# Two DMA streams moved from SyncE's queue to ScalarE's, and a planner that knows two TensorE clocks

## The chip, the cores and the metric

The kernel runs on one core of a Trainium2 chip. The metric is the device time of one execution in microseconds (us), as a median of several runs. A core has five engines that run side by side, each working through its own instructions in order: TensorE (PE, matrix products, with its weight loads shown as PEld), VectorE (DVE), ScalarE (ACT), GpSimd (POOL) and SyncE (SP, used here only to issue DMA transfers). They wait for each other by semaphores.

## The reference

The input x has shape 4 x 384 x 32 x 32 (batch, channels, height, width). Everything is float32. Layer 0 is a group norm followed by a selective scan in four directions; layer 1 is windowed attention and a mixture of four experts, of which each token uses two.

```
x = x + conv(group_norm(x))
    # conv: for each of 4 directions k and each of 384 channels d, with 16 states n:
    #   dt = softplus(dt_proj(x_proj(x)) + bias)
    #   h[n] = h[n] * exp(dt * A[n]) + dt * u * B[n]      (a scan over 1024 positions)
    #   y    = sum over n of h[n] * C[n]  + D * u
    # the four directions are added, then a layer norm and a gelu
t = tokens(x)                                   # 4 x 1024 tokens of 384
t = t + attention(layer_norm(t))                # 6 heads of 64, causal, 64 tokens back
t = t + experts(layer_norm(t))                  # top 2 of 4, hidden size 1536, gelu
```

## The kernel before

**The scan.** The 4 batches x 4 directions are 16 turns. A turn has 3 groups of 128 channels, and each of these is cut into 4 groups of 32. That makes 192 blocks of 32 channels. On the 128 partitions stand 32 channels times 4 states, so a block takes 4 slots for its 16 states, 768 slots in all. One slot is:

- `decay` (from line 772): ScalarE computes dA = exp(dt * A), 128 x 1024, into one of two tiles in PSUM (`das_`).
- `times_b` (756): POOL computes z = (dt * u) * B.
- `scan` (798): DVE scans h = dA * h + z along the 1024 positions.
- `times_c` (785): h is multiplied by C, on POOL or on DVE, whichever the planner thinks is free first.
- `fold_y` (828): when the four slots of a block are done, PE adds the 16 states of each channel by a product with the constant `fold` (output of 32 partitions), on top of the earlier value of y, loaded from DRAM as `yp`. ScalarE copies the sum back into `yp`, and a DMA stores it to `ydr`.

dt and dt * u are computed for 128 channels at a time by `time_steps` (689) and stored to a DRAM tile `dtr`. `spread(0)` and `spread(1)` (746) load them from there for each block of 32 channels, with each channel repeated on 4 partitions: `spread(0)` brings dt (for `decay`) into a stock of two tiles, `spread(1)` brings dt * u (for `times_b`) into another two. `state_rows` (677) loads the rows of B and C.

**Layer 1.** For each batch whose scan has ended, `front` (897), `attention` (956) and `route` (1161) run one after the other. Then `experts` (1296) runs over 19 blocks of 128 rows: for each, the hidden product (`ps_hid`, then a gelu on ScalarE into `hs`) and the output product (`y_ff`), with the weights loaded from DRAM for each block in 8 tiles. `combine` (1395) gathers the rows back. The layer 1 work of one batch is to run while the scan of the next is under way. The experts of a batch and its combination come last in priority.

**The order.** No order is written out by hand. Each of these parts is a Python generator that asks for one operation at a time, and a planner (`Machine`, line 201) decides in which order the instructions are emitted. It keeps a clock for each engine, adds a cost to it for each operation (`Engine.ask`, line 147), and remembers when each tile will be written and read. For each engine it picks, among the operations that can start by then, the one with the earliest start plus a bias (`EARLY` = -6 us, `LATER` = 6 us); for ScalarE it first prefers those that need no new activation table. The costs only decide the order; on the chip every engine runs what it was given in that order and waits where its inputs aren't there. Tiles come from stocks (`Stock.take` and `give`); three PSUM banks (`banks`) are shared by nearly all products. Planned start times of operations on SP get a margin of 1 us (`MARGIN`, `QUEUES`).

In the profile, all operations that go through `Engine.run` have line 137 and those of a list of calls (`Engine.all`) line 145.

Of the kernel before, what the change touches and what calls it, by code (L numbers as in the profile page):

```python
# [17 lines left out]
P = 128  # L18
# [50 lines left out]
class Stock:  # L69


    def __init__(self, m, pool, tag, n, shape):
        self.m, self.free = m, []
        self.tags, self.queue = {}, []
        self.add(pool, tag, n, shape)
# [32 lines left out]
class Op:  # L108


    def __init__(self, eng, outs, ins, cost, table, size):
        self.eng, self.outs, self.ins, self.cost, self.table, self.size = eng, outs, ins, cost, table, size


TABLES = {AF.Exp: "exp", AF.Ln: "ln", AF.Gelu: "gelu", AF.Sqrt: "sqrt"}
# [10 lines left out]
class Engine:  # L126
# [12 lines left out]
    def all(self, calls):  # L139

        asked = [self.ask(*c) for c in calls]
        outs, ins = ([ap for o in asked for ap in getattr(o, side)] for side in ("outs", "ins"))
        yield Op(self.name, outs, ins, sum(o.cost for o in asked), None, 0)
        for op, a, k in calls:
            getattr(self.real, op)(*a, **k)  # L145

    def ask(self, op, a, k):
        aps = [v for v in list(a) + [v for n, v in k.items() if n not in ("out", "accum_out")] if hasattr(v, "tensor")]
        if "out" in k:
            outs, ins = [k["out"]], aps  # L150
        else:
            outs, ins = aps[:1], aps[1:]
        if op == "value_load":
            outs, ins = [], aps
        if op == "tensor_tensor_reduce":
            outs, ins = outs + ins[-1:], ins[:-1]
        if k.get("accum_out") is not None:
            outs = outs + [k["accum_out"]]
        for v in list(k.values()):
            if isinstance(v, bass.IndirectOffsetOnAxis):  # L160
                ins = ins + [v.ap]
        n = max(v.free_size() if callable(v.free_size) else v.free_size for v in (outs if op == "matmul" else outs + ins))
        size, table = 0, None
        if "dma" in op:
            size = max(_nbytes(v) for v in outs + ins[:1])
            if op == "indirect_dma_start":
                size = P * D * 4
            cost = dict(pool=1.0, act=0.38, sp=0.48)[self.name]
        elif self.name == "pe":
            cost = max(n, 90) * (0.00122 if op == "transpose" else 0.00214)  # L170
            if outs[0].shape[0] == 32:
                cost *= 0.42
            if ins[0].shape[0] < 32:
                cost *= 0.6
        elif self.name == "act":
            cost = 0.08 + 0.00085 * n + 0.1 * sum(hasattr(k.get(v), "tensor") for v in ("bias", "scale"))
            cost += 0.19 if "accum_out" in k else 0.0
            table = TABLES.get(a[2]) if op == "activation" else None
        elif self.name == "pool":
            cost = 0.1 + 0.0022 * n  # L180
        elif self.name == "sp":
            cost = 1.5
        else:
            cost = 0.17 + 0.00198 * n if "scan" in op else 0.14 + 0.00105 * n
            if n < 256 and not any(v.space == PSUM for v in outs + ins):
                cost += 0.5
        return Op(self.name, outs, ins, cost, table, size)


def _nbytes(ap):  # L190
    n = 4
    for s in ap.shape:
        n *= s
    return n
# [6 lines left out]
class Machine:  # L201
# [4 lines left out]
    def __init__(self, nc):  # L206
        self.clock = dict(pe=0.0, act=0.0, dve=0.0, pool=0.0, sp=0.0)
        self.busy = dict(self.clock)
        self.written, self.read = {}, {}
        self.dram = {}  # L210
        self.dma, self.table, self.t, self.reach = 0.0, None, 0.0, 0.0
        self.pending = {e: [] for e in self.clock}
        self.waiting = []
        self.pe, self.act, self.dve = Engine(self, "pe", nc.tensor), Engine(self, "act", nc.scalar), Engine(self, "dve", nc.vector)
        self.pool, self.sp = Engine(self, "pool", nc.gpsimd), Engine(self, "sp", nc.sync)
# [31 lines left out]
    def settled(self, *tiles):  # L247

        names = [ap.tensor.name for ap in tiles]
        return lambda: max(self.written.get(n, (0.0, None))[0] for n in names) <= self.t + SOON  # L250

    def account(self, op, start):
        e = op.eng
        if op.table and op.table != self.table:
            start += TABLE_LOAD
            self.table = op.table
        end = start + op.cost
        self.busy[e] += end - max(self.clock[e], start)
        self.clock[e] = end
        if op.size:  # L260
            self.dma = max(self.dma, end) + op.size / DMA_RATE
            end = max(end + DMA_TIME, self.dma + 1.0)
            e = "dma"
        for aps, log, w in ((op.ins, self.read, False), (op.outs, self.written, True)):
            for ap in aps:
                name = ap.tensor.name
                if str(ap.space) .endswith("DRAM"):
                    self.dram.setdefault(name, []).append((*self.span(ap), end, w))
                elif log.get(name, (0.0, None))[0] <= end:
                    log[name] = end, e  # L270
        self.reach = max(self.reach, end)
# [77 lines left out]

PATIENCE = 3.0  # L350
SOON = 0.5
MARGIN, QUEUES = 1.0, ("sp",)


# [2 lines left out]
def conv_attn_hybrid(  # L357
# [146 lines left out]
    ydr = [dram.tile([T, JB, P, LQ], F32, tag="ydr", name="ydr") for _ in range(B)]  # L504
# [19 lines left out]
    pe, act, dve, pool, sp = m.pe, m.act, m.dve, m.pool, m.sp  # L524
# [221 lines left out]
    def spread(c):  # L746

        for n, (i, t, j) in enumerate(blocks):
            yield lambda: (i, t) in dtrs
            dst = yield from (dtus if c else dts).take("dts")  # L750
            yield from sp.dma_start(
                dst, dtrs[i, t][c, 32 * j : 32 * j + 32, :].unsqueeze(1).to_broadcast([32, SG, L])
            )
            spreads[n, c] = dst
# [43 lines left out]
    def scan():  # L798

        for s in range(NSLOT):  # L800
            n, g = divmod(s, NG)
            i = blocks[n][0]
            yield lambda: s in zs and s in das
            z, da = zs[s], das.pop(s)
            on_pool = count_of["times"] >= min(s + AHEAD, NSLOT) and m.clock["pool"] < m.clock["dve"] + LEAD
            h = z if on_pool else da
            if turns[i][1] >= 2:
                yield from dve.tensor_tensor_scan(
                    h[:, ::-1], da[:, ::-1], z[:, ::-1], 0.0, ALU.mult, ALU.add
                )  # L810
            else:
                yield from dve.tensor_tensor_scan(h, da, z, 0.0, ALU.mult, ALU.add)
            count_of["scan"] = s + 1
            if g == 0:
                m.spawn(fold_y(n), EARLY)
            if on_pool:
                das_.give(da)
                m.spawn(times_c(s, h, True))
            else:
                yield from times_c(s, h, False)  # L820
        ended.append(True)
        yield lambda: len(das_.free) == 2
        for stock in (banks, ybank):
            stock.free.append(das_.free.pop(0))
# [3 lines left out]
    def fold_y(n):  # L828


        i, t, j = blocks[n]
        b, k = turns[i]
        prev = yield from yps.take("yp")
        yield from sp.dma_start(prev, ydr[b][t, j])
        yield lambda: all(n * NG + g in ready for g in range(NG))
        yield m.settled(prev, *(zs[n * NG + g] for g in range(NG)))
        ps = yield from banks.take("ps_y", 0)
        y = ps[:, :LQ]
        mm = Calls()
        mm.matmul(y, ident, prev, start=True, stop=False)  # L840
        for g in range(NG):
            z = zs[n * NG + g]
            for q in range(4):
                if k % 2:
                    rhs = z.rearrange("p (w h) -> p h w", h=HH)[:, ts(q, HH // 4), :]
                else:
                    rhs = z[:, ts(q, LQ)]
                mm.matmul(y[32 * q : 32 * q + 32, :], fold, rhs, start=False, stop=g == NG - 1)
        yield from pe.all(mm)
        for g in range(NG):  # L850
            zs_.give(zs.pop(n * NG + g))
        yield from act.copy(prev, y)
        banks.give(ps)
        yield from sp.dma_start(ydr[b][t, j], prev)
        yps.give(prev)
        folded[b] = folded.get(b, 0) + 1
        if folded[b] == KG * NB:
            have.add(("scan", b))
# [656 lines left out]
```

## Time and profile before

Three runs took 4282.9, 4304.15 and 4314.34 us, median 4304.15 us. The profiled execution has a span of 4286.6 us.

| engine | busy us | share of the span | instructions |
|---|---|---|---|
| PE | 3167.0 | 74% | 19588 |
| PEld | 2064.0 | 48% | 19588 |
| DVE | 2925.7 | 68% | 2975 |
| ACT | 2293.2 | 53% | 3858 |
| POOL | 2769.1 | 65% | 1284 |

Issuing a DMA isn't counted as busy. The mean clock that PE was granted is 0.814 of full speed. The DMA engines moved 960.99 MB. In the profile a group of instructions is named by output tile, arrow, input tiles; "L137" and "L145" are the planner's lines, so the tile names tell the operations apart. A wait is written as engine, tile, arrow, and what came last before it could go on.

| DMA issues on SP | count | KB each |
|---|---|---|
| weights of the experts, `w_sb` | 608 | 576 |
| spreads, `dts` (both kinds) | 384 | 512 |
| rows of B and C, `bc` | 128 | 512 |
| loads of y, `yp` | 192 | 128 |
| stores of y, `ydr` | 192 | 128 |

A float32 product shows as two records, so 36 records of `ps_hid` are 18 products.

### The profile page before, as it was taken

What the parts mean: (1) busy time and instruction counts of PE and PEld (TensorE: products, weight loads), DVE (VectorE), ACT (ScalarE), POOL (GpSimd) and SP (SyncE); (2) the same over time, 40 slices, a digit from 0 to 9 for tenths busy, and PEclk for the clock granted to TensorE, in tenths of its full rate; (3) what the DMA queues carried; (4) which work ended last, traced back from release to release, by engine and by line L of the source; (5) the groups of instructions that cost most, each with busy time, mean ns of one, the idle gap of its engine ahead of it and who ended that gap; (6) DMA issues with size and microseconds to landing.
All of it is one profiled execution on the core that took longest, in us unless ns stands there. A gap on an engine that the chain in (4) does not pass through costs nothing.

```text
span 4286.6 us, 56954 instructions
## 1 busy us (share of the span) xinstructions
PE 3167.0 (74%) x19588; PEld 2064.0 (48%) x19588; DVE 2925.7 (68%) x2975; ACT 2293.2 (53%) x3858; POOL 2769.1 (65%) x1284
## 2 busy tenths in 40 slices
PE   2434344569955776687778856878999899998997
PEld 1111111235633443354455524545777677776785
DVE  2999999989898889998988999899621112211001
ACT  3555555676564777775667665886433234331221
POOL 1999999998888898998788988999500100002001
PEclk7566565578867898897778868889899899998997
DMA  5667563653457796765657777876349784397995
GB/s 191 208 238 237 185 231 130 195 196 122 141 193 290 259 320 216 248 237 168 214 173 272 247 242 245 310 264 213 120 127 334 266 298 126 119 335 261 309 320 168
DMA packets 450137, 960.99 MB, mean 224 GB/s; under 512 B 52980, under 2 KB 269304, under 8 KB 449848
## 3 DMA queue, kind: packets, MB, share of 16 engines
q1 hardware_dynamic: 441656, 932.17, 63.5%
q0 software_dynamic: 8192, 25.17, 1.7%
q8 instruction: 156, 2.56, 0.2%
q14 instruction: 133, 1.09, 0.1%
HBM read 805.46 MB, written 170.59 MB: 228 GB/s over the span
## 4 chain that ended last, share of the span: by engine, by line
PE 32%; DVE 10%; issue 5%; POOL 5%; ACT 5%; DMA 3%; SPq 0%; DVEq 0%; POOLq 0%; ACTq 0%
PE y_ff L145 9%; PE ps_hid L145 9%; POOL z L137 4%; DVE dA L137 4%; DVE z L137 3%; PE ps_y L145 2%; PE ps_o L145 2%; PE ps_c L145 2%; PE ps_qk L145 2%; ACT L137 1%; ACT dA L137 1%; PE ps_pr L145 1%; PE ps_p L145 1%; PE ps_v L145 1%; PE ps_s L145 1%
## 5 line engine op out<-in xcount | busy, mean ns | idle before, releaser
L137 POOL TENSOR_TENSOR z<-dts,bc 128x1024 f32<-128x1024 f32 x768 | 1797.6, 2370 | 158.6 <-ACT ps_sp L137 89.4
L137 ACT ACTIVATE dA<-dts,a 128x1024 f32<-128x1024 f32 x768 | 853.4, 1117 | 725.9 <-DVE z L137 697.3
L137 POOL TENSOR_TENSOR z<-z,bc 128x1024 f32<-128x1024 f32 x366 | 861.9, 2364 | 182.0 <-DVE z L137 161.8
L137 DVE TENSOR_TENSOR_SCAN dA<-dA,z 128x1024 f32<-128x1024 f32 x402 | 919.1, 2286 | 63.7 <-ACT dA L137 44.7
L145 PE MATMUL ps_y<-z,fold 128*32 128x256 f32 x6144 | 633.5, 556 | 303.2 <-POOL z L137 220.6
L137 DVE TENSOR_TENSOR_SCAN z<-dA,z 128x1024 f32<-128x1024 f32 x366 | 822.9, 2274 | 21.8 <-ACT dA L137 21.3
L145 PEld LDWEIGHTS ps_hid<-xbt,w_sb 128*128 128x128 f32 x5472 | 658.2, 199 | 50.2 <-issue 12.2
L145 PE MATMUL y_ff<-w_sb,hs 128*128 128x384 f32 x1824 | 662.6, 506 | 22.6 <-ACT hs L137 19.8
L145 PE MATMUL ps_hid<-xbt,w_sb 128*128 128x128 f32 x5472 | 668.7, 283 | 13.8 <-ACT dt L137 6.1
L145 PEld LDWEIGHTS ps_y<-z,fold 128*32 128x32 f32 x6144 | 203.9, 134 | 678.7 <-POOL z L137 296.6
L137 POOL DMA_INDIRECT xsdr<-tks,idx x64 | 63.3, 988 | 710.6 <-DMA tks<-tkdr 575.6
L137 DVE TENSOR_TENSOR z<-dA,bc 128x1024 f32<-128x1024 f32 x402 | 490.8, 1221 | 44.2 <-DMA bc<-xdr 22.9
L137 ACT ACTIVATE hs<-ps_hid,bb 128x128 f32<-128x128 f32 x912 | 265.7, 370 | 453.3 <-PE ps_hid L145 344.3
L145 PEld LDWEIGHTS y_ff<-w_sb,hs 128*128 128x128 f32 x1824 | 339.2, 197 | 238.7 <-issue 34.5
L145 PE MATMUL ps_y<-yp,ident 128*128 128x256 f32 x384 | 176.2, 551 | 346.7 <-ACT dt L137 172.4
L137 ACT ACT_TABLE_LOAD x315 | 404.1, 1283 | 34.4 <-DVE gs L137 11.8
L137 POOL DMA_INDIRECT cb<-ysdr,idx x64 | 62.0, 969 | 451.7 <-DMA cb<-t2dr 277.1
L145 PEld LDWEIGHTS ps_y<-yp,ident 128*128 128x128 f32 x384 | 77.6, 246 | 440.3 <-ACT dt L137 196.3
L137 DVE COPY yb<-y_ff 128x384 f32<-128x384 f32 x40 | 22.1, 554 | 299.7 <-PE y_ff L145 268.6
L145 PE MATMUL ps_dt<-xd,dtw_sb 12*128 12x512 f32 x192 | 100.2, 851 | 63.7 <-DMA dtw_sb<-in_dtw_dram 22.1
L145 PE MATMUL ps_o<-v,pt 128*128 128x64 f32 x720 | 143.8, 319 | 3.4 <-ACT pt L137 1.7
L145 PEld LDWEIGHTS ps_o<-v,pt 128*128 128x128 f32 x720 | 118.3, 207 | 31.9 <-ACT pt L137 2.6
(181 smaller groups left out, 3312.6 us busy)
## 6 DMA issues: line engine op xcount, KB each, us to landing
w_sb<-wl SPq DMA_DIRECT2D x608, 576.0 KB
dts<-dtr SPq DMA_DIRECT2D x384, 512.0 KB
bc<-xdr SPq DMA_DIRECT2D x128, 512.0 KB
ub<-udr SPq DMA_DIRECT2D x48, 512.0 KB
dtr<-e SPq DMA_DIRECT2D x48, 512.0 KB
dtr<-dt SPq DMA_DIRECT2D x48, 512.0 KB
yp<-ydr SPq DMA_DIRECT2D x192, 128.0 KB
ydr<-yp SPq DMA_DIRECT2D x192, 128.0 KB
```

Of the source, the lines that this page charges most:

```text
L137: return getattr(self.real, op)(*a, **k)
L145: getattr(self.real, op)(*a, **k)
```

## The change

It has two parts.

First, `spread` and the store at the end of `fold_y` are issued with `act.dma_start` in place of `sp.dma_start`. Both kinds of spread come from the same line, so all 384 spreads and all 192 stores of y move. The aim is to take waiting transfers out of SP's one queue.

Second, the planner's costs for PE change. Before, a product cost a fixed time per column. Now it has a cost at full clock and takes `COLD` = 1.9 times as long in a window of `WINDOW` = 3.413 us whose predecessor held less than a third of a window of work; the work of a product is counted by the share of the array's rows that it uses, and half for products with an output of 32 partitions. The aim is a plan whose PE times are nearer to the real ones, with an order that fits them.

```diff
@@ Engine.all
-        yield Op(self.name, outs, ins, sum(o.cost for o in asked), None, 0)
+        whole = Op(self.name, outs, ins, sum(o.cost for o in asked), None, 0)
+        whole.work = sum(o.work for o in asked)
+        yield whole
@@ Engine.ask
-            cost = max(n, 90) * (0.00122 if op == "transpose" else 0.00214)
+            cost = max(n, 90) * (0.00088 if op == "transpose" else 0.00176)
             if outs[0].shape[0] == 32:
-                cost *= 0.42
+                cost *= 0.51
             if ins[0].shape[0] < 32:
                 cost *= 0.6
...
-        return Op(self.name, outs, ins, cost, table, size)
+        asked = Op(self.name, outs, ins, cost, table, size)
+        if self.name == "pe":
+            asked.work = cost * min(ins[0].shape[0], P) / P if outs[0].shape[0] > 32 else 0.5 * cost
+        return asked
@@ Machine.__init__
-        self.dram = {}
+        self.dram, self.worked = {}, {}
@@ Machine.account
         end = start + op.cost
+        if e == "pe":
+
+            left, end = op.cost, start
+            while left > 0:
+                n = int(end / WINDOW)
+                f = 1.0 if self.worked.get(n - 1, 0.0) > WINDOW / 3 else COLD
+                step = min(left * f, (n + 1) * WINDOW - end + 1e-6)
+                self.worked[n] = self.worked.get(n, 0.0) + op.work * step / f / op.cost
+                left, end = left - step / f, end + step
@@ 
+WINDOW, COLD = 3.413, 1.9
@@ spread
-            yield from sp.dma_start(
+            yield from act.dma_start(
                 dst, dtrs[i, t][c, 32 * j : 32 * j + 32, :].unsqueeze(1).to_broadcast([32, SG, L])
             )
@@ fold_y
         yield from act.copy(prev, y)
         banks.give(ps)
-        yield from sp.dma_start(ydr[b][t, j], prev)
+        yield from act.dma_start(ydr[b][t, j], prev)
```

## The prediction

> **What bounds the kernel now.** I read the slices first, then the same engines by stage, then the waits of the DMA queue and the groups. The slices:
>
> ```profile
> PE   2434344569955776687778856878999899998997
> DVE  2999999989898889998988999899621112211001
> ACT  3555555676564777775667665886433234331221
> POOL 1999999998888898998788988999500100002001
> PEclk7566565578867898897778868889899899998997
> ```
>
> There are two regimes. Up to about 3070 us DVE and POOL run near full: the selective scan, 768 slots in four batches. After it PE runs near full, finishing what of attention and experts was not fitted in earlier. The stage view (stretch, then busy time of PE, weight loads, DVE, ACT, POOL, then clock) shows the size of the slack:
>
> ```profile
> 96.00:830.00 734.00, 306.68 (x1874) 95.62 (x1874) 709.16 (x483) 402.39 (x475) 702.29 (x305) 0.59 0.61 205
> 830.00:1600.00 770.00, 566.65 (x3578) 345.58 (x3577) 672.18 (x672) 508.87 (x788) 686.52 (x305) 0.81 0.62 215
> 1600.00:2340.00 740.00, 559.76 (x3565) 351.63 (x3566) 672.58 (x616) 505.08 (x794) 641.18 (x277) 0.82 0.63 214
> 2340.00:3070.00 730.00, 558.52 (x3675) 355.05 (x3674) 661.86 (x560) 495.15 (x754) 656.21 (x300) 0.84 0.71 246
> 3790.00:4230.00 440.00, 415.02 (x2454) 327.74 (x2452) 35.72 (x106) 100.22 (x320) 30.59 (x32) 0.96 0.85 292
> ```
>
> The first stage is full (DVE 709 of 734 us) and can't shrink. The next three leave DVE idle 98, 67 and 68 us: about 230 us is the most that better order could take out of the scan. PE is busy 75% there at a clock of 0.81 to 0.84, so it has room for expert work. How much it gets is seen in the windows of the output matmul alone (time, PE busy and count first):
>
> ```profile
> 830.00:1600.00 770.00, 60.07 (x168) 30.36 (x168) 1.61 (x3) 1.93 (x4) 0.81 0.62 215
> 1600.00:2340.00 740.00, 74.80 (x202) 36.94 (x203) 1.65 (x3) 2.38 (x5) 0.82 0.63 214
> 2340.00:3070.00 730.00, 121.39 (x315) 60.27 (x313) 2.73 (x5) 3.83 (x8) 0.84 0.71 246
> 3790.00:4230.00 440.00, 198.57 (x570) 106.01 (x570) 10.59 (x19) 2.39 (x5) 0.96 0.85 292
> ```
>
> A block of 128 rows takes 24 records of this matmul (1824 over 76 blocks). So 685/24 = 28.5 blocks, 38%, are done before the scan ends, and 47.5 after. In the last stage 570/24 = 23.75 blocks take 440 us: **18.5 us a block** is the price of each block left for the tail.
>
> The queue of SyncE, where all direct loads and stores now stand in one order, waits like this in the scan (total, times, longest):
>
> ```profile
> SPq L137 <- ACT yp L137: 506.4, 154, 19.0
> SPq L137 <- POOL z L137: 461.1, 176, 10.1
> SPq L137 <- ACT dA L137: 287.0, 112, 13.7
> ```
>
> The first is a store of y that waits for its copy. The second is a spread of dt * u that waits for POOL's products to free one of two buffers, the third a spread of dt that waits for the exponentials to free one. Every load behind them waits too. The engines that bound the scan see little of it: of their waits in that stretch, DVE puts 22.9 us to a load of the B and C rows, POOL 11.5 us to the same and 7.7 us to a spread.
>
> **What the Trainium skill says.** "DMA: Bandwidth & Descriptors", section "Issuing engines are not separate DMA queues": moving an issue to another engine saves only the issuing sequencer's time, since the same 16 DMA engines carry it. So I count nothing for bandwidth. The trace shows one queue row for all direct transfers, at 63.5% of the engines; a second row is not shown here. The same page, "Anatomy of one DMA": any wait happens on the issuing sequencer before dispatch. That agrees with the three rows above, and means the moved waits will now stand in ScalarE's stream. "TensorE: Matmul & The Clock Gate", Part 1: the array runs at half rate until it has been busy for a window of about 3.4 us. The trace agrees in direction: mean clock 0.59 in the first stage with little PE work, 0.96 in the last. The window itself isn't shown by the trace.
>
> **The change part by part.**
>
> *Moved issues.* Both kinds of spread come from one line, so 384 spreads and 192 stores of y leave SP for ScalarE. On SP one such issue has a median of 524 ns (spreads) and 337 ns (stores). SP loses 384 x 0.524 + 192 x 0.337 = 266 us of issuing and most of the 506 + 461 + 287 = 1254 us of waits. What was queued behind them, loads of tokens, weights, B and C rows, can go earlier. What it is worth: DVE's and POOL's waits on loads are 42 us by the rows above, and POOL waits 49.7 us for PE's folds to free z, some of which start late for a load of y (PE puts 21.0 us to that). I take half of the two, 45 us.
>
> *Cost on ScalarE.* No issue from ScalarE is in this trace. Lower end 0 (an issue hidden while an earlier activation runs). Upper end: SP's 266 us plus, for each store, a wait for the copy just before it, at most its 0.37 us (the copy group's mean) x 192 = 71 us, so 337 us. I take 266 us, 66 a stage: ScalarE goes from 68% (505 of 740) to about 77% in the full stages. Behind a stalled issue stands the next exponential, and behind that DVE's scan. A spread of dt costs no extra wait, since the exponential that frees its buffer runs on ScalarE itself. A spread of dt * u does: it waits for POOL, so ScalarE now hangs on POOL's pace wherever the real POOL runs behind the plan. But the exponentials have spare time: they sit 697 us waiting for DVE to free one of two dA buffers, and DVE waits just 44.7 + 21.3 = 66 us for them. I expose about a tenth, 30 us; at the upper end a third of 337, 112 us.
>
> *PE costs in the planner.* Old: 0.00214 us a column always. New: 0.00176 at full clock, 1.9 times that (0.00334) when the previous 3.413 us window held under a third of work. A block has 36 hidden products of 128 columns and 12 output products of 384, 9216 columns: planned 19.7 us before, 16.2 us after when warm. Measured in the trace: 36 records of the hidden product run in 4.02 us and 6 of the output in about 1.94 us, so 2 x 4.02 + 4 x 1.94 = 15.8 us warm. The old plan was 25% too slow for warm PE, and so left it idle in the real run between two folds; the new one is within 3%. A fold (32 columns out) is planned at 0.230 us in both when warm; cold it goes to 0.437 us, where 8 records (4 folds) take 1.08 us, 0.27 each. So cold folds become too dear in the plan, and this will push against experts in thin stretches. If all of the 18% that the plan thinks shorter went to experts, 28.5 blocks would become about 33.5, 5 more; I take half, 2.5 blocks x 18.5 = 46 us off the tail.
>
> *Tail order.* In 3070 to 4230 us PE is idle 260-270, 434-450, 415-440: 51 us. Loads planned with a PE that is 25% too slow come late; the pauses I saw were loads of weights around 3311, 3762 and 3770 us, 4.5 to 8 us each. I take 20 us.
>
> *The extra field and bookkeeping* run when the kernel is traced, before the chip: nothing.
>
> Sum: 4304 - 45 + 30 - 46 - 20 = 4223, say **4225 us**.
>
> **The rivals.**
>
> *Nothing gained (4295).* The scan is held by DVE and POOL work alone (709 and 702 of 734 us in the first stage), and what PE gets is set by the three PSUM banks and the order of attention, which the change leaves. For it: attention of the third batch ends only after the scan whatever the SP queue does. Against: 230 us of idle DVE isn't work. Time: 4304 - 10.
>
> *Slower (4400).* ScalarE becomes the stall: 112 us at the upper end, and little of the gains is left. For it: only two dA buffers stand between the exponentials and DVE; SP's 176 waits for POOL, 461 us, move into ScalarE's stream, where a plan that misjudges POOL turns each into a late exponential. Against: 697 us of slack. 4304 + 112 - 16 = 4400.
>
> *Much better (4110).* All 5 blocks fit in (93 us), DVE's idle time in the last three scan stages falls by a third (75 us), tail pauses go (26 us): 4304 - 194.
>
> **How the numbers follow.** Forecast 0.46, nothing gained 0.18, slower 0.21, much better 0.15. The order of some thousand instructions a stage is redone by the planner, so each case is spread by some 40 us; the three runs of before alone span 31 us. The range 4095 to 4365 takes the forecast, the middle case and most of the best, and leaves out most of the slower case and the far end of the best. Faster by over 1% (under 4261): all of the best and most of the forecast, 0.59. Within 1%: the middle case and some of the forecast, 0.21. Slower: 0.20.
>
> **What would show each step.** SP's waits on ACT yp, ACT dA and POOL z vanish and its issues fall by 576; ScalarE shows 576 issues of 0.3 to 0.55 us; DVE's waits on ACT dA stay under 100 us. More than 31 blocks of output matmuls stand before the scan's end, the scan ends by about 3050 us, and the tail falls from 1217 us to under 1170. I am wrong if DVE waits on ScalarE by 150 us or more, if the scan ends after 3100 us, or if fewer blocks than 28 fit in it.

## The result, and the profile after

The changed kernel takes 4473.39 us (median of four runs, 4465.72 to 4482.11), the kernel before 4296.47 us (4282.9 to 4314.34). The ratio is **1.041**, interval 1.0363 to 1.0457: slower by 4.1%, where 4225 us and a gain were forecast. The time lies above the range of 4095 to 4365 us.

The slices of the changed kernel:

```profile
PE   2434343568874775777777765578999999996997
DVE  3999999988889899999898979996220112221001
PEclk7556555678866886887788877788999999996997
```

The two regimes are the same, but PE's digits in the scan are lower (7s where there were 8s and 9s), and the PE-bound stretch behind it is longer. The views by stage, cut at the end of the scan (3056 us before, 3091 us after; that is where DVE starts its last instruction on `dA`), put sizes to it. What lies behind the scan is called the tail. First the kernel before, then the changed one; columns as in the prediction:

```profile
96.00:3056.00 2960.00, 1977.61 (x12555) 1137.55 (x12555) 2710.99 (x2314) 1906.91 (x2797) 2680.75 (x1182) 0.76 0.64 220
3056.00:4286.00 1230.00, 1159.58 (x6969) 913.97 (x6967) 194.36 (x615) 359.33 (x1028) 82.36 (x83) 0.93 0.69 237
```

```profile
96.00:3091.00 2995.00, 1904.89 (x11826) 1076.90 (x11827) 2717.25 (x2311) 1840.63 (x2670) 2625.83 (x1154) 0.74 0.60 206
3091.00:4473.00 1382.00, 1298.71 (x7698) 1024.70 (x7696) 213.31 (x654) 389.11 (x1119) 92.89 (x94) 0.92 0.70 237
```

The scan took 35 us longer and **the tail 152 us longer**. PE did 729 records less inside the scan, and they came back in the tail. Most of them belong to the experts, as the windows of the output matmul alone show, before and then after:

```profile
96.00:3056.00 2960.00, 256.26 (x684) 127.56 (x684) 5.98 (x11) 8.14 (x17) 0.76 0.64 220
3056.00:4286.00 1230.00, 406.33 (x1140) 211.66 (x1140) 16.17 (x29) 9.06 (x19) 0.93 0.69 237
```

```profile
96.00:3091.00 2995.00, 212.01 (x528) 104.04 (x528) 3.17 (x6) 7.67 (x16) 0.74 0.60 206
3091.00:4473.00 1382.00, 450.36 (x1296) 235.19 (x1296) 14.50 (x26) 13.38 (x28) 0.92 0.70 237
```

At 24 records a block that is 684/24 = 28.5 blocks of expert work inside the scan before and 528/24 = 22.0 after. Each engine runs in the order it was given, so this is no accident of the run: the same two numbers stand in the order that the planner wrote, in PE's stream ahead of the last fold. A block has 72 records of the hidden matmul and 24 of the output, so 6.5 blocks are 624 of the 729 records.

The moved issues did what was expected of them on their own queue. The DMA view of the changed kernel shows a second row, and the groups show 384 spreads at a median of 521 ns and 192 stores at 326 ns from ScalarE:

```profile
q1 hardware_dynamic: 358712, 705.64, 46.3%
q10 hardware_dynamic: 82944, 226.53, 14.8%
```

SP's waits (scan stretch of the changed kernel; total, times, longest) are new ones:

```profile
SPq L138 <- DVE e L138: 504.8, 46, 35.9
SPq L138 <- PE y_ff L148: 247.7, 51, 14.0
SPq L138 <- DMA ydr<-yp: 242.4, 39, 17.6
SPq L138 <- POOL z L138: 211.6, 66, 20.9
```

The two rows together hold the packets and bytes of the one row before (441656 and 932.17 MB), and they kept the 16 DMA engines busy for as long: 61.1% of 4473 us is 2733 us, and 63.5% of 4287 us was 2722 us. So the second row brought no bandwidth, as the Trainium skill has it in "DMA: Bandwidth & Descriptors", section "Issuing engines are not separate DMA queues": the transfers run on the same 16 engines, whichever engine issues them. SP's waits for the copies and the exponentials are gone. In their place SP now arrives early at stores that wait for dt * u, and at loads of y that wait for ScalarE's store of the same tile. Whether that hurts is told below by the last experiment.

### The profile page after: what moved, and what is told of

Same layout as the page of the kernel before. It is cut to its first block, busy times and chain, and to the rows that moved or that the text cites. A ratio compares the mean times of both kernels' runs of the same rounds, so it can differ in the third digit from the quotient of the medians.

```text
span 4473.3 us, 56930 instructions
## 1 busy us (share of the span) xinstructions
PE 3233.2 (72%) x19588; PEld 2114.1 (47%) x19588; DVE 2950.9 (66%) x3011; ACT 2256.0 (50%) x3820; POOL 2725.1 (61%) x1266
## 5 line engine op out<-in xcount | busy, mean ns | idle before, releaser
L138 DVE TENSOR_TENSOR_SCAN dA<-dA,z 128x1024 f32<-128x1024 f32 x420 | 960.6, 2287 | 84.4 <-ACT dA L138 69.5
L138 POOL TENSOR_TENSOR z<-z,bc 128x1024 f32<-128x1024 f32 x348 | 818.0, 2362 | 266.3 <-DVE z L138 241.0
L138 DVE TENSOR_TENSOR_SCAN z<-dA,z 128x1024 f32<-128x1024 f32 x348 | 781.8, 2274 | 22.2 <-ACT dA L138 21.5
L138 DVE TENSOR_TENSOR z<-dA,bc 128x1024 f32<-128x1024 f32 x420 | 512.6, 1221 | 35.4 <-DMA bc<-xdr 12.6
L138 ACT ACT_TABLE_LOAD x281 | 360.5, 1283 | 49.4 <-DVE gs L138 11.7
L138 DVE COPY xbt<-ps_xb 128x384 f32<-128x384 f32 x52 | 28.7, 553 | 433.8 <-PE ps_xb L148 433.8
```

Of the source, the lines that this page charges most:

```text
L138: return getattr(self.real, op)(*a, **k)
```

## The experiments

The theories, by the letters that the expectations use. **S**: ScalarE stalls on the moved issues. **C**: the cold clock in the plan does it all. **P**: what counts is how many expert blocks the order puts ahead of the scan's end, at 18.5 us each. **O**: the order costs, not the issuing engine. **F**: the overpriced cold fold makes the plan believe PE full. **K**: two clocks in a plan are bad in themselves. **R**: the order of before was tuned, and any reshuffle costs. **A**: the price of the moved issues in the plan. **N**: their lost margin. **M**: the old price of PE was a useful margin.

All ratios are to the kernel before, run on the same chip. "Blocks" are those ahead of the last fold in the order written, "scan ends" and "tail" are from each run's profile (a single execution).

| run | us | ratio (95%) | blocks | scan ends | tail |
|---|---|---|---|---|---|
| before | 4296 | 1 | 28.5 | 3057 | 1230 |
| changed | 4473 | 1.041 (1.036-1.046) | 22.0 | 3092 | 1382 |
| e1 moves alone | 4367 | 1.019 (1.015-1.024) | 23.75 | 3043 | 1312 |
| e2 PE model alone | 4412 | 1.029 (1.025-1.032) | 23.0 | 3028 | 1382 |
| e3 changed, one clock | 4380 | 1.022 (1.018-1.026) | 28.0 | 3107 | 1264 |
| e4 model, one clock | 4334 | 1.010 (1.006-1.014) | 28.5 | 3130 | 1209 |
| e5 order of before, on ScalarE | 4315 | 1.006 (1.003-1.009) | 28.5 | 3091 | 1236 |
| e6 order of changed, on SyncE | 4460 | 1.042 (1.040-1.045) | 22.0 | 3063 | 1384 |
| e7 model, fold price 0.32 | 4335 | 1.012 (1.009-1.014) | 29.75 | 3183 | 1152 |
| e8 changed, fold price 0.32 | 4451 | 1.039 (1.036-1.042) | 28.0 | 3200 | 1248 |
| e9 nudge of LEAD | 4286 | 0.999 (0.998-1.001) | 27.0 | 3024 | 1264 |
| e10 nudge of transposes | 4276 | 0.997 (0.996-0.998) | 27.5 | 3027 | 1247 |
| e11 moves free in the plan | 4364 | 1.017 (1.014-1.021) | 26.5 | 3077 | 1283 |
| e12 two clocks, dear PE | 4269 | 0.995 (0.993-0.997) | 27.25 | 3058 | 1202 |
| e13 moves with margin | 4376 | 1.020 (1.015-1.025) | 25.25 | 3090 | 1288 |
| e14 changed, dear PE | 4364 | 1.017 (1.013-1.022) | 26.5 | 3122 | 1248 |
| e15 stores alone | 4375 | 1.022 (1.017-1.026) | 25.5 | 3082 | 1281 |
| e16 spreads alone | 4382 | 1.024 (1.019-1.030) | 24.25 | 3080 | 1289 |
| e17 order of e1, on SyncE | 4352 | 1.014 (1.010-1.018) | 23.75 | 3031 | 1315 |
| e18 order of e12, on ScalarE | 4275 | 0.996 (0.995-0.998) | 27.25 | 3065 | 1213 |

### The two halves, and the clock (e1 to e4)

e1 makes only the two replacements of `sp.dma_start` by `act.dma_start` in the kernel before. e2 is the changed kernel with them undone. e3 and e4 are the changed kernel and e2 with

```diff
-WINDOW, COLD = 3.413, 1.9
+WINDOW, COLD = 3.413, 1.0
```

> Only the spreads and the stores of y are issued from ScalarE; the planner's PE costs are the old ones. In PE's emitted order 23.75 expert blocks stand ahead of the last fold (28.5 in the kernel before, 22.0 in the changed one). Theory P (placement: each expert block left behind the scan costs 18.5 us of tail): 4.75 blocks x 18.5 = 88 us over before, about 4385 us. Theory S (ScalarE stalls on the moved issues, the placement is a side effect): nearly the whole loss, about 4470 us, and the scan's end at 3095 us or later. Theory C (the cold clock in the planner does it all): about 4300 us.

> Only the new PE costs with the two clocks; all transfers stay on SyncE. 23.0 expert blocks stand ahead of the last fold. Theory P: 5.5 x 18.5 = 102 us over before, about 4400 us. Theory S: no loss, about 4300 us. Theory C: nearly the whole loss, about 4470 us.

> The changed kernel with COLD = 1.0: the new costs at full clock only, with the moved issues kept. 28.0 expert blocks stand ahead of the last fold. Theory P: 0.5 x 18.5 = 9 us over before, about 4305 us. Theory S: the loss stays, about 4450 us. Theory C: the loss goes, about 4300 us, so it is told from P by the two runs of one part alone.

> The new PE costs with COLD = 1.0, all transfers on SyncE. 28.5 expert blocks stand ahead of the last fold, 18.5 ahead of the third batch's last (14.75 before). Theory P: as before, about 4295 us, or some less since the batches before are further on. Theories S and C: about 4295 us.

Each half loses by itself, 1.9% and 2.9%, and together they lose 4.1%, about their sum (the intervals don't tell 4.1 from 4.8). C falls with e1, and S fails to explain e2, where ScalarE issues nothing. P got e1 (4367 for 4385) and e2 (4412 for 4400) nearly right, but not e3 (4380 for 4305) and e4 (4334 for 4295): there the blocks are back in the scan and the tail is short again (1264 and 1209 us), but **the scan has grown** to 3107 and 3130 us. So P tells half of it: a block put into the scan isn't free there.

### The same order, the other engine (e5, e6)

These plan a transfer for one engine and issue it from the other, so that no other instruction moves:

```diff
+        self.moved = Engine(self, "sp", nc.scalar)
...
-        yield from sp.dma_start(ydr[b][t, j], prev)
+        yield from m.moved.dma_start(ydr[b][t, j], prev)
```

and likewise for the spreads. e6 does the reverse to the changed kernel (`Engine(self, "act", nc.sync)`).

> The plan of the kernel before, with the same order on every engine, but the 384 spreads and 192 stores of y are issued from ScalarE at the places in time where the plan had them for SyncE. 28.5 blocks stand ahead of the last fold. Theory S (ScalarE stalls on the moved issues): a loss of 70 us or more, about 4370 us, with the scan's end later by as much. Theory O (the loss comes from the new order, not from the issuing engine): within 25 us of before, about 4300 us.

> The plan of the changed kernel, with the same order on every engine, but the moved transfers are issued from SyncE again. 22.0 blocks stand ahead of the last fold. Theory S: the loss from ScalarE goes, about 4400 us. Theory O: as the changed kernel or slower (SyncE has the waits back without a plan for them), 4470 to 4500 us.

S falls. 576 issues from ScalarE in an unchanged order cost 0.6%, 26 us; the order of the changed kernel costs the same 4.2% when SP issues everything. So the loss lies in the order. ScalarE's waits in e5 have two rows that the move brought (scan stretch; in the kernel before the first of these is 1.3 us and the second isn't there):

```profile
ACT dA L137 <- DMA dts<-dtr: 16.7, 5, 4.8
...
ACT dA L137 <- POOL z L137: 10.2, 3, 6.6
```

The first reads as exponentials that wait for a spread issued late, the second as exponentials behind a spread of dt * u that waits for POOL. That these two are the 26 us isn't shown: e18 (below) has 10.7 and 7.4 us in the same rows and loses nothing clear of the noise.

### What the plan believed (e7, e8)

The planner's own busy count of PE up to the last scan of the first batch (planned at 768 to 785 us), where PE does little but folds, can be set beside what PE was busy in the trace (96 to 830 us):

| kernel | planned PE busy | in the trace | blocks ahead of the last fold |
|---|---|---|---|
| before | 248 us | 307 us | 28.5 |
| e2 | 419 us | 307 us | 23.0 |
| e7 | 304 us | 313 us | 29.75 |

The new costs make a cold fold 0.437 us. In the trace of before, 8 records, which are 4 folds, take 1.08 us behind a pause, 0.27 each:

```profile
418.99 1.08 PE L145 MATMUL ps_y<-z,fold 128*32 128x256 f32 x8 [5.06 <-POOL z L137]
```

Over the whole kernel, all products into `ps_y` took 834 us in that trace. The plan of before booked 842 us for them, the plan of e2 1190. The new plan thus fills PE with fold time that isn't there, and holds expert work back. e7 and e8 are e2 and the changed kernel with a lower fold price, cold and warm:

```diff
-                cost *= 0.51
+                cost *= 0.32
```

> The new PE costs with both clocks, all transfers on SyncE, and only the factor for products with 32 output partitions changed from 0.51 to 0.32, so that a cold fold is planned at 0.274 us (measured 0.27) and not at 0.437. 29.75 blocks stand ahead of the last fold (23.0 with 0.51). Theory F (the overpriced cold fold made the plan believe PE full, and so pushed expert blocks behind the scan): tail 6.75 blocks x 18.5 = 125 us shorter than with 0.51, scan's end up to 80 us later as in the run with one clock, about 4330 us. Theory K (two clocks in the plan are bad in themselves): about 4410 us, as with 0.51.

> The changed kernel with only the factor for products with 32 output partitions changed from 0.51 to 0.32. 28.0 blocks stand ahead of the last fold (22.0 in the changed kernel). Theory F: 6 blocks x 18.5 = 111 us faster than the changed kernel, about 4360 us. Theory K or S: about 4470 us.

e7 gains 77 us over e2, with 6.75 more blocks inside the scan: K falls, and F holds for the model alone (4335 us where it gave 4330), though e7 is still 1.2% slower than before. The stage views show what it paid, first e2 and then e7:

```profile
96.00:3027.00 2931.00, 1866.27 (x11736) 1040.94 (x11737) 2709.81 (x2294) 1839.27 (x2633) 2600.14 (x1148) 0.75 0.62 212
3027.00:4410.00 1383.00, 1305.12 (x7788) 1028.72 (x7786) 224.02 (x695) 396.14 (x1147) 83.19 (x83) 0.93 0.68 231
```

```profile
96.00:3183.00 3087.00, 2105.58 (x13290) 1240.08 (x13291) 2717.54 (x2434) 1935.33 (x2903) 2695.41 (x1188) 0.76 0.62 214
3183.00:4335.00 1152.00, 1058.07 (x6234) 832.96 (x6233) 162.29 (x497) 314.36 (x904) 83.28 (x83) 0.91 0.72 246
```

The tail fell by 231 us, but the scan grew by 156, both about twice what F gave. DVE's work in it is the same (2710 and 2718 us), so its idle time went from 221 to 369 us. The reading is that a PE stream packed more tightly than PE can work it off holds DVE back; what supports it is the slip, the time by which the chip's scan ends later than the plan's. The plan of e7 ended the scan at 3057 us and the chip at 3183, a slip of 126 us; the plan of before slipped by 53 (3004 to 3057). For e8 F fails: its blocks are back at 28.0, yet it gained only 23 us. Its scan ends at 3200 us with a slip of 136.

### Controls (e9, e10)

```diff
-LEAD = 0.6
+LEAD = 0.61
```

```diff
-            cost = max(n, 90) * (0.00122 if op == "transpose" else 0.00214)
+            cost = max(n, 90) * (0.00121 if op == "transpose" else 0.00214)
```

> A control: the kernel before with LEAD = 0.61 in place of 0.6, a nudge without meaning that reshuffles the order. 27.0 blocks ahead of the last fold. If the order as such is tuned and any reshuffle costs (theory R): 4360 us or more. If only what the plan gets wrong costs (theories P and F): 1.5 blocks, 4315 us, give or take 25.

> A second control: the kernel before with a planned transpose cost of 0.00121 in place of 0.00122 us a column. 27.5 blocks ahead of the last fold. Theory R: 4360 us or more. Theories P and F: 1 block, 4305 us, give or take 25.

R falls for nudges of this size. They move the end of the scan and the tail by 17 to 34 us, in opposite directions, and the time by 0.3% at most. Two nudges that keep 27 and 27.5 blocks inside the scan don't show how much a larger reshuffle can cost, so for the larger changes R is not excluded. (e12 below is a larger one that cost nothing.)

### The price as a margin (e12)

e12 keeps the two clocks and all transfers on SP, and prices PE dear:

```diff
-            cost = max(n, 90) * (0.00088 if op == "transpose" else 0.00176)
+            cost = max(n, 90) * (0.00107 if op == "transpose" else 0.00214)
...
-                cost *= 0.51
+                cost *= 0.3
...
-WINDOW, COLD = 3.413, 1.9
+WINDOW, COLD = 3.413, 1.5
```

> All transfers on SyncE, two clocks in the plan, but PE priced as dear as before at full clock (0.00214, transposes 0.00107, folds factor 0.30, COLD 1.5). 27.25 blocks ahead of the last fold. Theory M (the old price was too dear for warm expert products and so left a margin for the narrow products that are priced too low; with the new price the real scan slips behind the plan): the scan ends within 70 us of the plan's 3021 us, as before, and the time is about 4310 us. Without M: a slip of 100 us or more, as with 0.00176, and about 4350 us.

M holds: a slip of 37 us (3021 to 3058), and 4269 us where it gave 4310, which is 3.3% less than e2. Against before it is 0.5% faster, which is little more than the 0.3% of the second nudge. Its stages:

```profile
96.00:3057.00 2961.00, 1979.81 (x12561) 1120.41 (x12562) 2702.20 (x2334) 1903.80 (x2804) 2667.56 (x1175) 0.76 0.64 218
3057.00:4259.00 1202.00, 1152.78 (x6962) 908.87 (x6962) 187.38 (x591) 360.06 (x1032) 81.96 (x82) 0.95 0.72 247
```

So with these prices the two clocks do no harm; that they help isn't shown. With the moves on ScalarE the same prices take 4451 us (e8) down to 4364 (e14), and the slip from 136 to 68. e12 changes three numbers against e7 at once, so that the price of warm work alone does it was not tried. What the three do together can be read from the planner, as the time that it books for PE over the whole kernel (SP issues all transfers in these five):

| kernel | PE booked in the plan | PE in the trace | slip of the scan |
|---|---|---|---|
| before | 3223 us | 3167 us | 53 us |
| e2 | 3269 us | 3201 us | 37 us |
| e12 | 3192 us | 3163 us | 37 us |
| e4 | 2753 us | 3187 us | 99 us |
| e7 | 2893 us | 3193 us | 126 us |

The slip goes with that sum. Where ScalarE issues transfers it is mostly larger, 43 to 87 us with a sum that is about right, and 92 and 136 us in e3 and e8, whose sums are as low as those of e4 and e7. That is a pattern over the runs and not a test of its own. The price of 0.00176 fits the experts, but other products take longer than their price, and the dear price made up for them in the sum: the products into `ps_o`, 64 columns each, were planned at 69 us even in before, and took 144. So what the old price gave is less a margin than a sum that is about right.

### The moves' own part (e11, e13 to e18)

e11 is e1 with `act=0.38` set to `act=0.0` in the planner's issue costs. e13 is e1 with

```diff
-        return MARGIN if bias and op.eng in QUEUES else 0.0
+        return MARGIN if bias and (op.eng in QUEUES or op.eng == "act" and op.size) else 0.0
```

e14 is the changed kernel with e12's prices, e15 and e16 make one of the two replacements in the kernel before. e17 and e18 are orders of e1 and e12, issued from the other engine as in e5 and e6.

> The spreads and stores moved, the old PE costs, and the planner's cost of a transfer issued from ScalarE set from 0.38 to 0 us. 26.5 blocks ahead of the last fold (23.75 with 0.38). Theory A (576 x 0.38 = 219 us of ScalarE time that the plan now books for the early work pushes the gelus, and with them the expert blocks, back): 2.75 blocks x 18.5 = 51 us better than the moves alone, about 4320 us. Otherwise (what counts is where the issues stand, not what they are priced): 4365 us as the moves alone.

> The moves alone, old PE costs, and the planner's margin of 1 us kept for transfers that ScalarE issues for early or late work. 25.25 blocks ahead of the last fold (23.75 without it). Theory N (the moved transfers lost their cushion, so that ScalarE's order stalls on them): 4330 us or less. Otherwise about 4365 us as the moves alone.

> The changed kernel with the PE prices of the run with a dear PE and two clocks (0.00214, transposes 0.00107, folds factor 0.30, COLD 1.5). 26.5 blocks ahead of the last fold, planned end of the scan 3054 us. Theory M (the prices carry the model's part of the loss, the moves theirs): the moves' 76 us on top of 4270 us, about 4345 us, and a slip of the scan of 80 us at most. If the two parts of the change don't add up: 4420 us or more.

> Only the 192 stores of y moved, old PE costs. 25.5 blocks ahead of the last fold. Theory P: 3 blocks x 18.5 = 55 us, about 4340 us. If the spreads carry the moves' loss (they wait for POOL): about 4295 us.

> Only the 384 spreads moved, old PE costs. 24.25 blocks ahead of the last fold. Theory P: 4.25 blocks x 18.5 = 79 us, about 4365 us. If the stores carry the moves' loss: about 4300 us.

> The plan of the moves alone (old PE costs), with the same order on every engine, but the spreads and stores are issued from SyncE again. 23.75 blocks ahead of the last fold. Theory O (the order carries the moves' loss, ScalarE's own share is about 25 us): about 4340 us. Theory S (the issuing engine carries it): about 4290 us.

> The plan of the run with a dear PE and two clocks, same order on every engine, but the spreads and stores are issued from ScalarE. 27.25 blocks ahead of the last fold. Theory O: ScalarE's own share of 25 to 35 us on 4269 us, about 4300 us, all of it ahead of the scan's end, tail as it was (1202 us). Theory S: 4350 us or more.

A and N fall: neither the price nor the margin alone brings anything back, though both put more blocks inside the scan than e1. Either stream alone costs as much as both, more than P gives for it. With e12's PE prices the moves still cost 2.3% (e14 to e12). And the four orders that ran on both engines split it:

| order of | issued by SP | issued by ScalarE |
|---|---|---|
| before | 1 | 1.006 |
| changed | 1.042 | 1.041 |
| e1 | 1.014 | 1.019 |
| e12 | 0.995 | 0.996 |

ScalarE's own share is between nothing and 0.6% of the time. (The scan did end later in all four profiles, by 7 to 34 us.) The rest of the moves' loss, 1.4% in e17, is the order that the planner writes once it books these transfers for ScalarE. e18 also clears SP's new waits. They are all there (scan stretch of e18),

```profile
SPq L138 <- DVE e L138: 424.3, 44, 29.8
SPq L138 <- PE y_ff L148: 247.7, 62, 14.4
...
SPq L138 <- DMA ydr<-yp: 174.4, 28, 18.1
```

and the run is as fast as e12, which has none of these rows as long. **What in the planner turns the moved booking into a worse order stays open.** Price and margin, each alone, are excluded; that the freed SP stream itself lets other work in too early was not tried, nor was a reshuffle of the same size without the moves. One thing narrows it: this loss is one that the planner's own clocks already show. Its plan for before ends at 4351 us, for e1 at 4456, for e15 and e16 at 4431 and 4444. So the moves led a planner that picks one operation at a time to a plan that is longer by its own costs. It is no proof of a loss on the chip: the nudges' plans end at 4392 and 4378 us and cost nothing. For e2 it was the other way: its plan ends at 4338 us, and the chip didn't follow it.

## Why the prediction was wrong

Two steps failed. The larger one is **PE costs in the planner**: "-46 us" for 2.5 more expert blocks inside the scan. The model alone went the other way: it put 5.5 blocks *fewer* there (23.0 for 28.5) and cost 2.9%, 121 us. The text had the reason in it, that "cold folds become too dear in the plan", with both prices, 0.437 us planned for 0.27 measured, but set no time against the gain for it beyond taking half. On 16 folds a block of channels and 192 such blocks it is no small term: the plan booked 1190 us for the products into `ps_y`, where the trace has 834. e7 shows that this price alone holds back 6.75 blocks.

A second error lies in the same step. The old price of an expert block, 19.7 us for 15.8 measured warm, was called a fault that left PE idle. It stood against prices of other products that are too low, so that the old plan's sum for PE was right (3223 us for 3167). e7 and e12 show what follows: with a price that fits the experts and is too low for others, the scan slips 126 us behind its plan, with the dear one 37.

The other step is **moved issues** with its cost on ScalarE, -45 + 30 = -15 us. Moving them cost 1.9%, 76 us (e1). The order that the planner would write for them stood in the text as a spread of some 40 us around each case, not as a loss; by e17 it is 1.4%, and its cause stays open.

- *Moved issues, -45 us*: not found. SP's waits for the copies and the exponentials went as said, and that for POOL halved. But the waits of DVE and POOL on loads fell only from 42 to 21 us (without the wait of 89 us ahead of POOL's first product, which both kernels have), and POOL's wait for folds didn't fall at all (49.7 and 53.5 us). In e5, with the order of before, the move gained nothing. Other waits took their place in SP's queue, and e18 shows that they cost nothing either.
- *Cost on ScalarE, +30 us*: of the right size. Same order, other engine: between about nothing and +26 us, with whatever the move gained in it. DVE's waits for the exponentials went from 66 to 91 us in the changed kernel (the two rows below), under the 100 named, and the issues took 521 and 326 ns.

```profile
DVE dA L138 <- ACT dA L138: 69.5, 44, 5.0
DVE z L138 <- ACT dA L138: 21.5, 19, 2.3
```

- *Price of a block left for the tail, 18.5 us*: mis-sized. A line through the 20 profiles, tail against blocks left, has a slope of some 24.5 us (correlation 0.92). Attention and the rest fall behind with the blocks: e2's tail has 247 us more of PE than e7's, and only 120 of them are the experts' two products.
- *Tail order, -20 us*: not found. The tail ran at 25.9 us per block left before (1230/47.5) and 25.6 after (1382/54).
- *The rivals*: "slower" had the side but not the cause; ScalarE did not become the stall. The sign named as fatal, fewer than 28 blocks inside the scan, is what came.
- The range ended at 4365 us and the time fell 108 us above it. The slower case was built from ScalarE alone; a new order that is plainly worse had no case.

## What to carry to other kernels

When a planner's costs are changed, compare its booked time for each engine, stage by stage and in sum, with the trace before trusting the new order: here one price, 60% too high on one operation, made the plan believe an engine full. A price that is too high for one operation can stand against others that are too low. Making that one exact by itself took the sum 9% below what PE really did (2893 us for 3193 in e7), so correct the others with it. And to tell what an issuing engine costs from what a new order costs, run the same order on both engines.

## What the runs showed that wasn't expected

Issuing 576 transfers from an engine that is busy for some 64% of the scan cost next to nothing in four orders (0.6% at most), although in the changed kernel those issues took 384 x 0.521 + 192 x 0.326 = 263 us. Part of it ran beside ScalarE's own work, as here in the changed kernel, where an issue starts 0.03 us after an exponential of 1.14 us:

```profile
2018.79 1.14 ACT L138 ACTIVATE dA<-dts,a 128x1024 f32<-128x1024 f32 x1
2018.82 0.52 ACTq L138 DMA_DIRECT2D dts<-dtr  x1
```

And filling idle PE time in the scan isn't free: from e2 to e7, 239 us of PE work came into the scan (1866 to 2106), which lengthened it by 156 us, and so gave back two thirds of the 231 us that the tail lost.
